# PSUM of a transformer stage as one tile of eight banks, and a new order of its steps

## The chip, the core and the metric

The kernel runs on one core of a Trainium2 chip. The core has TensorE (PE; its weight loads are shown apart as PEld), VectorE (DVE), ScalarE (ACT), GpSimd (POOL) and SyncE (SP, which here only issues DMAs). Each engine works through its own queue in order and waits on semaphores for the others. TensorE writes into PSUM, which has 8 banks of 512 float32 per partition; VectorE and ScalarE read it from there. The metric is the device time of one execution in microseconds, lower is better; it is given as the median of several runs.

## The reference, cut to what matters

Sixteen sequences of 256 tokens with 128 features go through two blocks. Block 0 is full attention, then a six-layer local transformer; block 1 is a state-space layer and a linear layer. The change lies in the local transformer:

```python
for i in range(DEPTH):                       # 6 layers
    x = attn_layer(shift_tokens(x), Wqkv[i], q_scale[i], k_scale[i], Wo[i]) + x
    x = ffn_layer(shift_tokens(x), ln_g[i], ln_b[i], W1[i], b1[i], W2[i], b2[i]) + x

def attn_layer(x, Wqkv, qs, ksc, Wo):        # 16 heads of 64
    q, k, v = heads(x @ Wqkv)
    q, k = rotary(l2norm(q) * qs), rotary(l2norm(k) * ksc)
    # a window of 32 queries sees its own 32 keys and the 32 before, masked
    return local_attention(q, k, v) @ Wo

def ffn_layer(x, g, bln, W1, b1, W2, b2):
    a, gate = split(layernorm(x) * g + bln) @ W1 + b1
    return a * gelu(gate) @ W2 + b2
```

`shift_tokens` delays half of the features by one token. All of it is float32.

## The kernel before

The tokens stay on the chip as `F`, features on the partitions. Class `Transformer` computes the six layers; a group is two sequences (512 tokens), so a layer has 8 groups and the stage 48. Work is cut into small steps, each a method that issues a few instructions on one engine. `ORDER` lists the steps of one period: `Pq00@0` is step P with the arguments q, 0, 0 for the period's own group, `FM2@3` is step FM with argument 2 for the group three periods earlier. `run` goes through this list once per group, so `ORDER` fixes the order of every engine's queue. `TAIL` lists by hand what is left after the 48th period, and the first steps of the state-space stage (`@s`), for which `Early` borrows the stage's tiles.

The steps, by engine. The arguments are q or k, the sequence b of the group, and the half t of its 256 tokens.

- TensorE. P (L628): q or k for 128 tokens, two matmuls of 512 columns. T (L702): transposes the rotated q or k, 16 pieces on 64 rows. X (L729): transposes F to tokens, as values. S (L759): scores, 64 small matmuls on 64 rows, added to the mask. G (L817): probabilities times values, 8 matmuls on 32 rows. Y (L838): four of the 16 heads times the product of Wv and Wo. F1, F5 (L858, L894): transposes round the layer norm. FP (L914) and FY (L938): the feed-forward matmuls. `value_output` (L608): makes the product of Wv and Wo of the next layer, half of it in each of a layer's last two periods, and copies it out with ScalarE.
- VectorE. C (L644) and N (L656): products with the cosine and sine tables, read from P's tile. R (L668): sums of squares. RR (L686): reciprocal. MX (L772) and SB (L778): maximum of the scores, and its subtraction. SM (L791): sums. TP (L805): transposes probabilities. FADD (L848), FF (L951), F2, FM: residual sums, statistics, gate. In the last layer FF has four more products (L960).
- ScalarE. Q (L638): squares of P's tile. E (L719): copies a transpose to SBUF. K (L746): writes the mask into the scores' tile. EX (L787): exponential. B (L828): copies G's result. W (L732): copies X's tile to SBUF. F4, F6, FE, SQ.
- POOL. A (L675): sum of C's and N's products. M (L690): times the reciprocal norm. NR (L798): times 1/sum. MXS, F3, FN.
- SP. V: two DMAs a sequence that shift the values by one window.

PSUM is shared out by two `Slots` objects: three tiles of two banks (`two`: for P, T, S, G, FP and `value_output`) and two of one bank (`one`: X, Y, F1, F5, FY). `take` gives the slot that has been free longest; `drop` counts a tile's readers and frees it after the last one. The instruction that writes a slot next waits for the last reader of the tile before.

Of the kernel before, what the change touches and what calls it, by code (L numbers as in the profile page):

```python
# [10 lines left out]
F32 = mybir.dt.float32  # L11
# [6 lines left out]
P = 128  # L18
B, S, D = 16, 256, 128
# [3 lines left out]
NG = B // G  # L23
# [8 lines left out]
DEPTH, HEADS, DH, W = 6, 16, 64, 32  # L32
PAIRS = HEADS // 2
INNER = HEADS * DH
FF = int(D * 4 * 2 / 3)
# [423 lines left out]


ORDER = """
Pq00@0 FM2@3 Cq00@0 Nq000@0 EX01@1 Mq10@1 Mk10@1 SM01@1 EX00@1 G10@2 Qq000@0 FADD0@2 B101@2 B100@2
Ak11@1 FY@3 Nq001@0 Aq00@0 SM00@1 Qq001@0 Rq00@0 G11@2 B111@2 FF@3 Mq11@1 X0@1 Pk01@0 Ck01@0 Tk10@1
B110@2 Pq01@0 Nk010@0 Nk011@0 W0@1 Ek10@1 Qk010@0 Cq01@0 Qk011@0 Pk00@0 Ak01@0 Tq10@1 V0@1 Qk000@0
Qk001@0 Nq010@0 Nq011@0 Aq01@0 NR00@1 Y10@2 Eq10@1 Y11@2 Qq010@0 Qq011@0 Rk01@0 Rk00@0 NR01@1 Ck00@0
K10@1 Nk000@0 Rq01@0 MXS0@0 Mk11@1 Tq11@1 Eq11@1 S10@1 Nk001@0 TP00@1 Ak00@0 Pq11@0 MX10@1 SB10@1
SQ0@0 Qq110@0 Nq110@0 Nq111@0 Cq11@0 Pq10@0 Qq100@0 Qq101@0 Tk11@1 Y12@2 Qq111@0 Nq100@0 Nq101@0
Cq10@0 Ek11@1 Y13@2 FADD1@2 G00@1 K11@1 B000@1 S11@1 TP01@1 B001@1 X1@1 G01@1 RR0@0 EX10@1 Aq10@0
MX11@1 Mk00@0 SB11@1 F1@2 F2@2 B010@1 B011@1 Mq00@0 W1@1 EX11@1 Rq10@0 Mq01@0 Pk10@0 Pk11@0 Qk110@0
Tk00@0 Ek00@0 F3@2 FN@2 F4@2 Ck10@0 Nk100@0 Nk101@0 Ck11@0 Aq11@0 V1@1 Y00@1 Tq00@0 Eq00@0 Y01@1  # L470
Tq01@0 F5@2 Qk100@0 Y02@1 Qk101@0 K00@0 SM11@1 F6@2 Mk01@0 SM10@1 S00@0 Eq01@0 Tk01@0 Rk10@0 Nk110@0
Nk111@0 NR11@1 TP11@1 Qk111@0 MX00@0 SB00@0 Ek01@0 FP0@2 FE0@2 Rk11@0 K01@0 FP1@2 NR10@1 Y03@1
Rq11@0 MXS1@0 FE1@2 FM0@2 FM1@2 Ak10@0 SQ1@0 TP10@1 RR1@0 S01@0 MX01@0 FP2@2 FE2@2 SB01@0
"""

TAIL = """
Ak11@0 Mk10@0 X0@0 FADD0@1 Mk11@0 W0@0 G10@1 FM2@2 L1@s B101@1 Mq11@0 G11@1 EX00@0 B110@1 B111@1  # L480
ST@s B100@1 Mq10@0 FY@2 Tq11@0 AG@s Tk10@0 Tk11@0 SM00@0 Eq11@0 Tq10@0 FF@2 Ek10@0 RS@s NB@s Y10@1
K11@0 Ek11@0 EX01@0 Y11@1 NR00@0 S11@0 V0@0 TP00@0 Y12@1 Eq10@0 SM01@0 MX11@0 Y13@1 XN@s L2@s SB11@0
K10@0 G00@0 FADD1@1 X1@0 EX11@0 SM11@0 S10@0 HT@s NR01@0 F1@1 B001@0 TP01@0 MX10@0 SB10@0 B000@0
NR11@0 W1@0 PX1@s U1@s G01@0 B010@0 PX0@s F2@1 B011@0 TP11@0 V1@0 Y00@0 F3@1 EX10@0 FN@1 Y01@0 G11@0
U0@s SM10@0 Y02@0 NR10@0 TP10@0 F4@1 Y03@0 PD@s B111@0 B110@0 XD@s WB@s G10@0 B100@0 B101@0 PZ1@s
F5@1 FADD0@0 ZA1@s F6@1 PZ0@s ZA0@s EE@s WW@s Y10@0 W2@s Y11@0 Y12@0 Y13@0 ZR1@s FADD1@0 FP0@1 F1@0
ZR0@s FP1@1 LL@s FP2@1 FE1@1 LW@s F2@0 FE0@1 F3@0 ZF@s FM1@1 FM0@1 FE2@1 FN@0 DU@s F4@0 FM2@1 F5@0
FY@1 F6@0 FP1@0 FP2@0 FP0@0 FE1@0 FF@1 FE2@0 TB@s FM1@0 FM2@0 FE0@0 FM0@0 FY@0 CB@s FF@0 MS@s
"""


class Slots:


    def __init__(self, pool, tag, n):
        self.pool, self.tag, self.free, self.held = pool, tag, list(range(n)), {}

    def take(self, shape, name, uses=1):
        i = self.free.pop(0)
        t = self.pool.tile(shape, F32, tag=f"{self.tag}{i}", name=name, bufs=1)  # L500
        self.held[id(t)] = [t, i, uses]
        return t

    def drop(self, t):
        h = self.held[id(t)]
        h[2] -= 1
        if h[2] == 0:
            self.free.append(h[1])
            del self.held[id(t)]


class Transformer:
# [36 lines left out]
    def pools(self, ctx, m):  # L549
        tc = self.c.tc  # L550
        self.m = m
        self.sb = ctx.enter_context(tc.tile_pool(name="lts", bufs=2))
        ps = ctx.enter_context(tc.tile_pool(name="ltp", bufs=1, space=PSUM))
        self.two = Slots(ps, "two", 3)
        self.one = Slots(ps, "one", 2)
        self.su, self.sw = Slots(self.sb, "u", 7), Slots(self.sb, "w", 4)
        self.spp, self.spT, self.sqT = (Slots(self.sb, k, 2) for k in ("pp", "pT", "qT"))

        self.kT = self.sb.tile([P, PAIRS, W + S], F32, tag="kT", name="kT", bufs=1)
        self.c.nc.gpsimd.memset(self.kT[:, :, 0:W], 0.0)  # L560
        self.at = self.sb.tile([P, HEADS, S], F32, tag="at", name="at", bufs=1)

        self.xw = []
        for b in range(G):
            t = self.sb.tile([P, NT, 2, D], F32, tag=f"xw{b}", name=f"xw{b}", bufs=1)
            self.c.nc.gpsimd.memset(t[0:W, 0, 0, :], 0.0)
            self.xw.append(t)
# [29 lines left out]
    def value_output(self, i, jh):  # L597

        nc, l = self.c.nc, self.layers[i]
        if jh == 0:  # L600
            l.wvo = self.wp.tile([P, HEADS, D], F32, tag="wvo", name="wvo")
        pw = self.two.take([P, 2, 4, D], "pw")
        for j in range(4):
            for e in range(2):
                es = slice(e * DH, (e + 1) * DH)
                jj = jh * 4 + j

                nc.tensor.matmul(  # L608
                    pw[:, e, j, :],
                    l.wv[es, jj, :],  # L610
                    l.wo[es, jj, :],
                    start=(j == 0),
                    stop=True,
                    skip_group_check=True,
                )
        for e in range(2):
            o = e * PAIRS + jh * 4
            nc.scalar.copy(l.wvo[:, o : o + 4, :], pw[:, e])
        self.two.drop(pw)
# [353 lines left out]
    def run(self):  # L973
        steps = []
        for o in ORDER.split():
            name, lag = o.split("@")
            base = name.rstrip("0123456789") if name[0] != "F" or name[:2] == "FA" else name
            steps.append((name, int(lag)))
        last = max(lag for _, lag in steps)
        groups = {}  # L980
        n = DEPTH * NG
        for jh in range(2):
            self.value_output(0, jh)
        for p in range(n):
            i, j = divmod(p, NG)
            if j == last + 1 and i + 1 < DEPTH:
                self.load(i + 1)
            if j >= NG - 2 and i + 1 < DEPTH:
                self.value_output(i + 1, j - NG + 2)
            if p == n - 4:  # L990
                self.early.load()
            groups[p] = self.group(p)
            for name, lag in steps:
                if p >= lag:
                    self.step(name, groups[p - lag])
            groups.pop(p - last, None)
        for o in TAIL.split():
            name, k = o.split("@")
            if k == "s":
                self.early.step(name)  # L1000
            else:
                self.step(name, groups[n - 1 - int(k)])
# [704 lines left out]
```

## Time and profile before

| | |
|---|---|
| runs | 3850.8, 3852.3, 3856.6 us; median 3852.29 |
| span of the profiled execution | 3847.4 us |
| mean granted TensorE clock | 0.987 |
| full attention, up to the first step of the local stage | about 430 us |
| 48 periods of the local stage | from about 430 to 3250 us |
| steady groups: 711.1 to 2946.1 us | 38 groups, PE busy 2217.0, DVE 2117.2, ACT 1711.0, POOL 1647.1 us |
| TAIL and the state-space stage | from 3250 us on |

The profile is one execution, with the start and the length of every instruction. A row of the timeline is start, length, engine, line, operation, output and inputs, shape, and how many equal instructions follow each other; in brackets stands idle time of the engine before it and what ended it. Lengths of TensorE rows are modelled and overlap, so the distance between the starts of two rows says more than the length of one. A float32 matmul leaves two MATMUL records and two weight loads, a transpose one of each. A row of waits is: engine, line, what it waited for, then microseconds in total, times, and the longest. "issue" stands for waiting for nothing that the profile shows.

### The profile page before, as it was taken

How to read it: one execution, taken by the hardware profiler on the slowest of the kernel's cores; microseconds unless marked ns; L12 is line 12 of the kernel's file. 1: busy time of each engine (PE TensorE's matmuls, PEld its weight loads, DVE VectorE, ACT ScalarE, POOL GpSimd, SP SyncE). 2: the span in 40 equal slices, each digit the busy share in tenths (PEclk: the TensorE clock that was granted, in tenths of full speed). 3: DMA queues.
4: the chain of work that ended last, by engine and by line, in shares of the span. 5: the costliest groups of instructions: out<-in, count | busy, mean ns of one | idle time of the engine just before them, and what ended most of it. 6: DMA issues, size and time to landing. Idle time of an engine off the chain costs nothing.

```text
span 3847.4 us, 104054 instructions
## 1 busy us (share of the span) xinstructions
PE 3693.1 (96%) x45040; PEld 2197.4 (57%) x45040; DVE 3385.9 (88%) x4736; ACT 2820.0 (73%) x4009; POOL 2603.6 (68%) x1636
## 2 busy tenths in 40 slices
PE   8999689999999999999999999999999999899997
PEld 4445355665655656666556656566665556555554
DVE  4665489999999999999999999999999999599997
ACT  3565467777777777777777777777777777689895
POOL 2222477777777777777777777777777776388887
PEclk9999789999999999999999999999999999999999
DMA  1000001000010000100001000010000000243432
GB/s 54 8 7 5 1 7 34 6 5 7 6 34 5 7 6 6 35 6 6 5 7 34 5 6 7 6 34 7 6 6 5 20 7 6 82 117 104 123 109 71
DMA packets 85669, 97.21 MB, mean 25 GB/s; under 512 B 9416, under 2 KB 56668, under 8 KB 84444
## 3 DMA queue, kind: packets, MB, share of 16 engines
q1 hardware_dynamic: 85212, 90.56, 8.5%
q8 instruction: 355, 5.82, 0.6%
q14 instruction: 102, 0.84, 0.1%
HBM read 75.32 MB, written 3.94 MB: 21 GB/s over the span
## 4 chain that ended last, share of the span: by engine, by line
PE 65%; DVE 20%; issue 2%; POOL 1%; ACT 1%; DVEq 0%; POOLq 0%; ACTq 0%
PE py L838 16%; PE pq L628 11%; PE pa L817 7%; PE fp L914 7%; PE s L759 6%; PE pt L702 5%; DVE w L656 3%; PE y L1361 3%; DVE u L644 3%; DVE ss L668 3%; PE db L1345 2%; DVE sm L791 2%; DVE s L1351 2%; PE px L1202 1%; DVE F L951 1%
## 5 line engine op out<-in xcount | busy, mean ns | idle before, releaser
L675 POOL TENSOR_TENSOR u<-u,w 128x1024 f32<-128x1024 f32 x384 | 907.2, 2367 | 405.2 <-DVE w L656 218.3
L690 POOL TENSOR_TENSOR u<-u,r 128x1024 f32<-128x1024 f32 x384 | 724.5, 1903 | 19.1 <-DVE r L686 16.6
L838 PE MATMUL py<-at,wvo 128*128 128x256 f32 x3072 | 736.5, 388 | 0.1
L628 PE MATMUL pq<-wqk,F 128*128 128x512 f32 x1536 | 715.6, 604 | 9.4 <-ACT sq L638 3.3
L638 ACT ACTIVATE sq<-pq 128x512 f32<-128x512 f32 x768 | 432.8, 601 | 301.3 <-PE pq L628 157.3
L838 PEld LDWEIGHTS py<-at,wvo 128*128 128x128 f32 x3072 | 569.6, 192 | 103.2 <-issue 23.2
L644 DVE TENSOR_TENSOR u<-pq,cosl 128x1024 f32<-128x1024 f32 x384 | 466.6, 1215 | 46.2 <-PE pq L628 43.1
L656 DVE TENSOR_TENSOR w<-pq,sinl 128x512 f32<-128x512 f32 x768 | 499.4, 681 | 8.9 <-ACT sq L638 2.1
L828 ACT COPY at<-pa 128x1024 f32<-128x1024 f32 x384 | 368.6, 1012 | 162.9 <-PE pa L817 157.9
L668 DVE TENSOR_REDUCE ss<-sq 128x16 f32<-128x1024 f32 x384 | 451.5, 1196 | 6.2 <-ACT sq L638 6.2
L628 PEld LDWEIGHTS pq<-wqk,F 128*128 128x128 f32 x1536 | 277.0, 191 | 296.2 <-issue 257.2
L817 PE MATMUL pa<-pT,xw 32*128 32x512 f32 x3072 | 411.8, 620 | 5.5 <-ACT sq L638 2.1
L798 POOL TENSOR_TENSOR pp<-pp,sm 128x1024 f32<-128x1024 f32 x192 | 363.8, 1916 | 50.3 <-DVE sm L794 50.3
L702 PEld LDWEIGHTS pt<-ident,u 64*128 64x128 f32 x6144 | 223.7, 139 | 227.0 <-issue 81.8
L1351 DVE TENSOR_TENSOR_SCAN s<-da,db 128x512 f32<-128x512 f32 x256 | 301.1, 1207 | 21.2 <-PE db L1345 9.3
L759 PEld LDWEIGHTS s<-kT,qT 64*32 64x32 f32 x24576 | 257.0, 106 | 90.0 <-issue 79.2
L759 PE MATMUL s<-kT,qT 64*32 64x64 f32 x24576 | 290.3, 227 | 16.4 <-issue 11.3
L702 PE MATMUL pt<-ident,u 64*128 64x64 f32 x6144 | 275.5, 230 | 29.4 <-ACT sq L638 10.6
L772 DVE TENSOR_REDUCE mx<-s 128x16 f32<-128x1024 f32 x192 | 230.5, 1200 | 69.7 <-PE s L759 67.2
L252 DVE TENSOR_REDUCE mx<-s 128x2 f32<-128x512 f32 x256 | 165.3, 687 | 139.9 <-PE sT L280 121.5
L817 PEld LDWEIGHTS pa<-pT,xw 32*128 32x128 f32 x3072 | 180.2, 186 | 172.6 <-issue 76.8
L914 PE MATMUL fp<-hT,w 128*128 128x512 f32 (+1 forms) x576 | 270.7, 606 | 0.0
(223 smaller groups left out, 6269.3 us busy)
## 6 DMA issues: line engine op xcount, KB each, us to landing
btd<-bc SPq DMA_DIRECT2D x72, 512.0 KB
bte<-bc SPq DMA_DIRECT2D x56, 256.0 KB
xw<-xw SPq DMA_DIRECT2D x96, 96.0 KB
wqk<-in_Wqk SPq DMA_DIRECT2D x6, 1024.0 KB
wv<-in_LWvT SPq DMA_DIRECT2D x6, 512.0 KB
wo<-in_Wo SPq DMA_DIRECT2D x6, 512.0 KB
xin<-in_x SPq DMA_DIRECT2D x8, 256.0 KB
out<-ot SPq DMA_DIRECT2D x8, 256.0 KB
```

What stands on the lines that cost most here:

```text
L628: nc.tensor.matmul(q.p[:, x], self.F[:, g.b0 + b, o : o + P], g.l.wqk[:, k, x, :], start=True, stop=True)
L638: self.c.nc.scalar.activation(q.sq[:, x], q.p[:, x], AF.Square)
L644: self.c.nc.vector.tensor_tensor(q.u.rearrange("p h x d -> p x h d"), q.p, g.l.cosl[:, t, k].unsqueeze(2).to_broadcast([P, 2, HEADS, DH // ...
L656: self.c.nc.vector.tensor_tensor(q.w[:, :, x], q.p[:, 1 - x], g.l.sinl[:, t, k, x, :].unsqueeze(1).to_broadcast([P, HEADS, DH // 2]), ALU. ...
L668: self.c.nc.vector.tensor_reduce(g.ss[b][:, t, k, :], q.sq.rearrange("p x h d -> p h x d"), AX.XY, ALU.add)
L675: self.c.nc.gpsimd.tensor_tensor(q.u, q.u, q.w, ALU.add)
L690: self.c.nc.gpsimd.tensor_tensor(uf, uf, g.r[b][:, t, k, :].unsqueeze(2).to_broadcast([P, HEADS, DH]), ALU.mult)
L702: self.c.nc.tensor.matmul(q.pt[:, r, j, :], uf[rs, j * P : (j + 1) * P], self.c.ident[rs, rs], is_transpose=True, start=(j == 0), stop=Tru ...
L759: nc.tensor.matmul(s[qs, e, j, :], qT[es, j, qs], kT[es, j, ks : ks + 2 * W], start=False, stop=True, skip_group_check=True,)
L817: self.c.nc.tensor.matmul(g.pa[b, t, w // 2][:, w % 2, :], self.xw[b][qs, t, k, :], g.pT[b, t][qs, k, :], start=(k == 0), stop=(k == 1),)
L838: self.c.nc.tensor.matmul(g.py[b], g.l.wvo[:, h, :], self.at[:, h, :], start=(h == 0), stop=(h == HEADS - 1),)
L914: self.c.nc.tensor.matmul(p[0:n, x, :], g.l.w1[:, w : w + n], g.hT, start=True, stop=True)
```

## The change

PSUM of the local stage becomes one tile of eight banks. A two-bank tile takes a free pair of banks (an even one and the next), the pair that has been free longest; a one-bank tile takes a free bank, by preference one whose neighbour is in use. `value_output` is split into its matmuls (step PW) and its copies (step PC), which get places in the order. `ORDER` and `TAIL` are new lists of the same steps: places within an engine's queue change, and seven steps change their lag (X0, W0 and Ak11 from 1 to 0, FADD0 from 2 to 1, FM2 from 3 to 2, FM0 from 2 to 3, RR1 from 0 to 1).

```diff
 ORDER = """
-Pq00@0 FM2@3 Cq00@0 Nq000@0 EX01@1 Mq10@1 Mk10@1 SM01@1 EX00@1 G10@2 Qq000@0 FADD0@2 B101@2 B100@2
...
-Cq10@0 Ek11@1 Y13@2 FADD1@2 G00@1 K11@1 B000@1 S11@1 TP01@1 B001@1 X1@1 G01@1 RR0@0 EX10@1 Aq10@0
-MX11@1 Mk00@0 SB11@1 F1@2 F2@2 B010@1 B011@1 Mq00@0 W1@1 EX11@1 Rq10@0 Mq01@0 Pk10@0 Pk11@0 Qk110@0
-Tk00@0 Ek00@0 F3@2 FN@2 F4@2 Ck10@0 Nk100@0 Nk101@0 Ck11@0 Aq11@0 V1@1 Y00@1 Tq00@0 Eq00@0 Y01@1
-Tq01@0 F5@2 Qk100@0 Y02@1 Qk101@0 K00@0 SM11@1 F6@2 Mk01@0 SM10@1 S00@0 Eq01@0 Tk01@0 Rk10@0 Nk110@0
-Nk111@0 NR11@1 TP11@1 Qk111@0 MX00@0 SB00@0 Ek01@0 FP0@2 FE0@2 Rk11@0 K01@0 FP1@2 NR10@1 Y03@1
-Rq11@0 MXS1@0 FE1@2 FM0@2 FM1@2 Ak10@0 SQ1@0 TP10@1 RR1@0 S01@0 MX01@0 FP2@2 FE2@2 SB01@0
+PW@0 PC@0 Pq00@0 G10@2 EX01@1 FM0@3 RR1@1 Nq000@0 Cq00@0 SM01@1 X1@1 Qq000@0 Qq001@0 Mk10@1 Nq001@0
+B101@2 Rq00@0 FY@3 B100@2 G11@2 EX00@1 B111@2 Pk01@0 B110@2 FF@3 SM00@1 Nk010@0 Qk010@0 W1@1 Pk00@0
+Mq11@1 Aq00@0 Mq10@1 Ck01@0 Tq10@1 Tk10@1 Nk011@0 Qk011@0 Qk000@0 Mk11@1 Ek10@1 Ak01@0 NR00@1 Pq01@0
+Nk000@0 Rk01@0 Ck00@0 Y10@2 Nk001@0 Eq10@1 Qq010@0 Y11@2 Cq01@0 Nq010@0 Qk001@0 Tq11@1 Nq011@0 K10@1
+Qq011@0 Rk00@0 NR01@1 Tk11@1 TP00@1 Eq11@1 Rq01@0 S10@1 V0@1 Pq10@0 MX10@1 MXS0@0 Y12@2 SQ0@0 Ek11@1
+RR0@0 SB10@1 V1@1 Nq100@0 Qq100@0 Y13@2 Ak00@0 Nq101@0 EX10@1 Aq01@0 Cq10@0 Mq01@0 FADD1@2 Pq11@0
+G00@1 TP01@1 Nq110@0 Qq101@0 K11@1 Qq110@0 S11@1 Aq10@0 Qq111@0 B000@1 Nq111@0 Tq01@0 Cq11@0 B001@1
+Mk01@0 Eq01@0 MX11@1 SB11@1 G01@1 SM10@1 F1@2 Mk00@0 X0@0 F2@2 B010@1 Rq10@0 W0@0 Mq00@0 B011@1
+Pk10@0 Qk100@0 Qk101@0 F3@2 EX11@1 Y00@1 Ck10@0 Nk100@0 Y01@1 FN@2 Nk101@0 Tq00@0 Tk00@0 Tk01@0 F4@2
+F5@2 Eq00@0 Ek00@0 F6@2 Pk11@0 Rk10@0 Aq11@0 Ek01@0 Ak10@0 SM11@1 FP2@2 Rq11@0 FP1@2 Nk110@0 Nk111@0
+FE2@2 Ck11@0 Y02@1 NR11@1 TP11@1 Qk110@0 Qk111@0 FM2@2 NR10@1 K00@0 K01@0 FE1@2 Rk11@0 S00@0 S01@0
+Y03@1 TP10@1 FM1@2 Ak11@0 MX00@0 MXS1@0 MX01@0 SQ1@0 SB00@0 SB01@0 FADD0@1 FP0@2 FE0@2
 """
...
+class Banks:
+    def __init__(self, t):
+        self.t, self.n = t, t.shape[1]
+        self.user, self.since, self.clock, self.held = [0] * self.n, list(range(self.n)), self.n, {}
...
+    def pair(self):
+        free = [b for b in range(0, self.n, 2) if not self.user[b] and not self.user[b + 1]]
+        return min(free, key=lambda b: max(self.since[b], self.since[b + 1]))
+
+    def single(self):
+        free = [b for b in range(self.n) if not self.user[b]]
+        split = [b for b in free if self.user[b ^ 1]]
+        return min(split or free, key=lambda b: self.since[b])
...
-        self.two = Slots(ps, "two", 3)
-        self.one = Slots(ps, "one", 2)
+        banks = Banks(ps.tile([P, 8, 512], F32, tag="banks", name="banks"))
+        self.two, self.one = Banked(banks, 2), Banked(banks, 1)
...
-            if j >= NG - 2 and i + 1 < DEPTH:
-                self.value_output(i + 1, j - NG + 2)
...
-                if p >= lag:
+                if name in ("PW", "PC"):
+                    if j >= NG - 2 and i + 1 < DEPTH:
+                        value = self.value_output if name == "PW" else self.value_output_copy
+                        value(i + 1, j - NG + 2)
+                elif p >= lag:
                     self.step(name, groups[p - lag])
```

`Banked` has `Slots`' interface (`take`, `drop`): it marks the banks that it takes as used and gives out a view of the one tile. `TAIL` has to finish what `ORDER` leaves over, so with the lags it loses Ak11@0, FADD0@1, FM2@2, W0@0 and X0@0 and gains FM0@2 and RR1@0; its other steps are those of before, in a new order.

On TensorE one period reads, before: Pq00 G10 FY G11 X0 Pk01 Tk10 Pq01 Pk00 Tq10 Y10 Y11 Tq11 S10 Pq11 Pq10 Tk11 Y12 Y13 G00 S11 X1 G01 F1 Pk10 Pk11 Tk00 Y00 Tq00 Y01 Tq01 F5 Y02 S00 Tk01 FP0 FP1 Y03 S01 FP2. After: (PW) Pq00 G10 X1 FY G11 Pk01 Pk00 Tq10 Tk10 Pq01 Y10 Y11 Tq11 Tk11 S10 Pq10 Y12 Y13 Pq11 G00 S11 Tq01 G01 F1 X0 Pk10 Y00 Y01 Tq00 Tk00 Tk01 F5 Pk11 FP2 FP1 Y02 S00 S01 Y03 FP0.

More of the change, by code (lines that the diff above doesn't have):

```diff
@@ L461 @@
 ORDER = """
-Pq00@0 FM2@3 Cq00@0 Nq000@0 EX01@1 Mq10@1 Mk10@1 SM01@1 EX00@1 G10@2 Qq000@0 FADD0@2 B101@2 B100@2
[L463 to L466, printed above, removed]
@@ L467 @@
-SQ0@0 Qq110@0 Nq110@0 Nq111@0 Cq11@0 Pq10@0 Qq100@0 Qq101@0 Tk11@1 Y12@2 Qq111@0 Nq100@0 Nq101@0
-Cq10@0 Ek11@1 Y13@2 FADD1@2 G00@1 K11@1 B000@1 S11@1 TP01@1 B001@1 X1@1 G01@1 RR0@0 EX10@1 Aq10@0
-MX11@1 Mk00@0 SB11@1 F1@2 F2@2 B010@1 B011@1 Mq00@0 W1@1 EX11@1 Rq10@0 Mq01@0 Pk10@0 Pk11@0 Qk110@0
-Tk00@0 Ek00@0 F3@2 FN@2 F4@2 Ck10@0 Nk100@0 Nk101@0 Ck11@0 Aq11@0 V1@1 Y00@1 Tq00@0 Eq00@0 Y01@1
-Tq01@0 F5@2 Qk100@0 Y02@1 Qk101@0 K00@0 SM11@1 F6@2 Mk01@0 SM10@1 S00@0 Eq01@0 Tk01@0 Rk10@0 Nk110@0
-Nk111@0 NR11@1 TP11@1 Qk111@0 MX00@0 SB00@0 Ek01@0 FP0@2 FE0@2 Rk11@0 K01@0 FP1@2 NR10@1 Y03@1
@@ L474 @@
+FE2@2 Ck11@0 Y02@1 NR11@1 TP11@1 Qk110@0 Qk111@0 FM2@2 NR10@1 K00@0 K01@0 FE1@2 Rk11@0 S00@0 S01@0
+Y03@1 TP10@1 FM1@2 Ak11@0 MX00@0 MXS1@0 MX01@0 SQ1@0 SB00@0 SB01@0 FADD0@1 FP0@2 FE0@2
 """
 TAIL = """
-Ak11@0 Mk10@0 X0@0 FADD0@1 Mk11@0 W0@0 G10@1 FM2@2 L1@s B101@1 Mq11@0 G11@1 EX00@0 B110@1 B111@1
-ST@s B100@1 Mq10@0 FY@2 Tq11@0 AG@s Tk10@0 Tk11@0 SM00@0 Eq11@0 Tq10@0 FF@2 Ek10@0 RS@s NB@s Y10@1
-K11@0 Ek11@0 EX01@0 Y11@1 NR00@0 S11@0 V0@0 TP00@0 Y12@1 Eq10@0 SM01@0 MX11@0 Y13@1 XN@s L2@s SB11@0
@@ L483 @@
[L483 to L487, printed above, removed]
@@ L488 @@
-FY@1 F6@0 FP1@0 FP2@0 FP0@0 FE1@0 FF@1 FE2@0 TB@s FM1@0 FM2@0 FE0@0 FM0@0 FY@0 CB@s FF@0 MS@s
+FM0@2 V0@0 G11@1 B111@1 B110@1 G10@1 B101@1 B100@1 L1@s FY@2 RR1@0 Mq10@0 Mk11@0 EX01@0 ST@s AG@s
+RS@s NB@s Mq11@0 Y10@1 FF@2 Y11@1 X1@0 EX00@0 Tq10@0 XN@s SM01@0 W1@0 V1@0 SM00@0 Mk10@0 NR01@0
+Tk10@0 Tq11@0 Eq11@0 Eq10@0 Ek10@0 TP01@0 L2@s HT@s NR00@0 Y12@1 Y13@1 FADD1@1 Tk11@0 G01@0 K10@0
+S10@0 Ek11@0 B011@0 TP00@0 G00@0 B010@0 K11@0 S11@0 B001@0 F1@1 MX10@0 SB10@0 EX10@0 SM10@0 MX11@0
+F2@1 F3@1 FN@1 B000@0 PX0@s U0@s NR10@0 PX1@s Y00@0 U1@s PD@s SB11@0 EX11@0 Y01@0 SM11@0 NR11@0
@@ L489 @@
+TP11@0 XD@s WB@s Y02@0 Y03@0 TP10@0 F4@1 G11@0 FADD0@0 G10@0 B110@0 TB@s F5@1 B111@0 B100@0 CB@s
+B101@0 PZ1@s ZA1@s PZ0@s ZR0@s ZA0@s EE@s F6@1 WW@s LL@s Y10@0 W2@s Y11@0 Y12@0 LW@s Y13@0 FADD1@0
+FP1@1 F1@0 F2@0 F3@0 ZR1@s ZF@s FP2@1 FE2@1 FE1@1 FP0@1 FM1@1 FE0@1 FN@0 F4@0 F5@0 FM0@1 FM2@1 FY@1
+FF@1 F6@0 FP2@0 FE2@0 FP1@0 FE1@0 FM1@0 DU@s MS@s FP0@0 FE0@0 FM2@0 FM0@0 FY@0 FF@0
 """
@@ L509, in drop, with view, __init__, take @@
             del self.held[id(t)]
+class Banks:
+    def __init__(self, t):
+        self.t, self.n = t, t.shape[1]
+        self.user, self.since, self.clock, self.held = [0] * self.n, list(range(self.n)), self.n, {}
+    def view(self, b, n, shape):
+        t = self.t[0 : shape[0], b : b + n, :].rearrange("p b x -> p (b x)")[:, 0 : int(np.prod(shape[1:]))]
+        if len(shape) > 2:
+            names = "abc"[: len(shape) - 1]
+            keys = dict(zip(names, shape[1:]))
+            t = t.rearrange(f"p ({' '.join(names)}) -> p {' '.join(names)}", **keys)
+        return t
+    def pair(self):
[5 more added lines that the diff above has]
+        return min(split or free, key=lambda b: self.since[b])
+class Banked:
+    def __init__(self, banks, n):
+        self.banks, self.n = banks, n
+    def take(self, shape, name, uses=1):
+        k = self.banks
+        b = k.pair() if self.n == 2 else k.single()
+        for i in range(b, b + self.n):
+            k.user[i] = 1
+        t = k.view(b, self.n, shape)
+        k.held[id(t)] = [t, b, uses]
+        return t
+    def drop(self, t):
+        k = self.banks
+        h = k.held[id(t)]
+        h[2] -= 1
+        if h[2] == 0:
+            for i in range(h[1], h[1] + self.n):
+                k.user[i], k.since[i] = 0, k.clock
+            k.clock += 1
+            del k.held[id(t)]
 class Transformer:
@@ L601, in value_output @@
             l.wvo = self.wp.tile([P, HEADS, D], F32, tag="wvo", name="wvo")
-        pw = self.two.take([P, 2, 4, D], "pw")
+        pw = l.pw = self.two.take([P, 2, 4, D], "pw")
         for j in range(4):
@@ L615, in value_output, with value_output_copy @@
                 )
+    def value_output_copy(self, i, jh):
+        nc, l = self.c.nc, self.layers[i]
+        pw = l.pw
         for e in range(2):
@@ L983, in run @@
             self.value_output(0, jh)
+            self.value_output_copy(0, jh)
         for p in range(n):
```

## The prediction

> **What bounds the kernel now.** I read the page first (shares and queues), then the busy time of each engine in a steady stretch of the local stage, the chain of waits over one group, the timeline of TensorE, and last the waits.
>
> ```profile
> PE 3693.1 (96%) x45040; PEld 2197.4 (57%) x45040; DVE 3385.9 (88%) x4736; ACT 2820.0 (73%) x4009; POOL 2603.6 (68%) x1636
> ...
> PEclk9999789999999999999999999999999999999999
> ...
> q8 instruction: 355, 5.82, 0.6%
> ```
>
> The reader is to see a TensorE at full clock that is never idle, a VectorE not far behind it, and a queue that carries instructions: 90,080 matmuls and weight loads in 355 packets (5.82 MB, so 16.4 KB each); one packet is some 254 of them (the built program has 91,052 with its waits: 256 each).
>
> The busy times from 1000 to 1290.5 us (five groups) are PE 287.9, DVE 275.3, ACT 221.7, POOL 216.0: per group 57.6, 55.1, 44.3, 43.2. A group takes 58.1: the `u` product of step Cq00 starts at 2829.8 and, two groups later, at 2946.1.
>
> ```profile
> 1002.92 1.73 PE pq L628 x4
> 1004.67 1.23 DVE u L644
> ...
> 1025.35 1.12 DVE mx L772
> 1026.49 1.24 DVE pp L778
> 1027.86 0.28 PE pt L702 x2
> ...
> 1061.23 1.73 PE pq L628 x4
> 1062.99 1.22 DVE u L644
> ```
>
> This is the chain of waits. It is a loop: 23.2 us of VectorE (Cq00 to SB10, 1004.67 to 1027.86), then 35.1 us of TensorE (Tk11 to the next Pq00). The hand-over back is a PSUM wait: Tk11 needs a two-bank tile, and the third is held by the scores that SB10 reads. TensorE is almost full by itself: that wait costs it only 0.2 us a group (`pt <- DVE pp` below).
>
> ```profile
> 1018.23 3.72 PE L838 MATMUL py<-at,wvo 128*128 128x256 f32 x16
> 1043.00 2.00 PE L838 MATMUL py<-at,wvo 128*128 128x256 f32 x8
> 1044.93 0.71 PE L702 MATMUL pt<-ident,u 64*128 64x64 f32 x16
> 1048.63 1.89 PE L838 MATMUL py<-at,wvo 128*128 128x256 f32 x8
> ...
> 1550.04 1.42 PE L759 MATMUL s<-kT,qT 64*32 64x64 f32 x120
> 1552.91 0.32 PE L759 MATMUL s<-kT,qT 64*32 64x64 f32 x8 [1.45 <-issue]
> ```
>
> ```profile
> PE s L759 <- issue: 8.5, 8, 1.8
> PE pt L702 <- DVE pp L778: 4.8, 21, 0.2
> ```
>
> Two things are to be seen. Changing the array's shape costs time: 16 `py` records between two transposes last 3.65 us (1018.23 to the next start, 1021.88), 8 last 1.93 (1043.00 to 1044.93). So 8 more cost 1.72, and the two ends of such a stretch 1.93 - 1.72 = 0.21. And TensorE sometimes stops inside a run of scores with nothing to wait for but its next instructions. At 1552.91 a packet of q8 had started at 1550.52 and landed at 1551.60; and the stop, after 240 of the run's 256 instructions, is at a multiple of 256 of TensorE's program (instruction 239 of the run).
>
> **The change, part by part.** I use S for scores, T for transposes, G, Y, P, FP as the steps are named; "full" is a matmul on the whole array (P, X, Y, FY, F1, F5, FP), "split" one on 64 or 32 rows (T, S, G).
>
> *PSUM as eight banks.* No compute instruction is added. In the built program TensorE's separate waits fall from 903 to 460, VectorE's rise from 633 to 734, ScalarE's from 579 to 641, POOL's from 673 to 765. Such a wait is an EVENT_SEMAPHORE row of 28 ns (median of ten before L732): 101 x 0.028 = 2.8 us on VectorE over the whole run, off the path while VectorE has 3 us free a group. Tk11 no longer waits for SB10 (in the new program it waits for Nq011, Qq011 and Mk11): -0.2 us a group.
>
> *The order on TensorE.* Same matmuls, but the full ones stand together. Before, a group has 13 stretches of full work between split work: FP2-Pq00, FY, X0-Pk01, Pq01-Pk00, Y10-Y11, Pq11-Pq10, Y12-Y13, X1, F1-Pk10-Pk11, Y00, Y01, F5-Y02, FP0-FP1-Y03. After, 7: Y03-FP0-Pq00, X1-FY, Pk01-Pk00, Pq01-Y10-Y11, Pq10 to Pq11, F1 to Y01, F5 to Y02. 6 x 0.21 = -1.26. Split steps next to each other (T beside S: 0.64 and 1.41 whatever stands next; T beside G isn't in the trace) I cost at nothing; bounds -0.1 and +0.25, the gap between the slow and fast G (1.93 and 2.18). TensorE alone would then need 58.1 - 0.2 - 1.26 = 56.6 us a group.
>
> *The order on the others.* VectorE's 55.1 stay. The moves (FADD0, RR1 and the FM/FP steps change places and lags, X0 and W0 go to the group's own period) add no instruction. V0's and V1's two DMAs still have SP's queue to themselves; W0 now stands some 20 us of TensorE work ahead of V0. The longest loop through several engines that I find in the new order is MX01, SB01 and on to Nq110 on VectorE (32.4), Qq111 and B000 on ScalarE (2.4), Tq01 to S01 on TensorE (20.8): 55.6. So nothing but TensorE binds, with 1 us to spare, and that 1 us hides every other edit; if it goes, VectorE's gaps (2.4 us a group now) come on top.
>
> *What the new order costs: the supply of instructions.* S00 and S01 now follow each other: 128 matmuls, 512 instructions, in 2.82 us. Any 512 hold a whole block of 256, gone in 1.41 us. From the packets and matmul starts in the trace: deep in a run of scores, the next packet starts 0.9 us after a block's first instruction and lands at 2.0, and after the stops TensorE resumes 1.4 after landing. That is 3.3 us against 1.41: a stop of 1.9. The seven large ones between 660 and 3000 us were 1.3 to 1.8 (mean 1.56, their block held a few transposes as well). Where a block starts within about 9 matmuls of the run's begin, the packet starts 0.8 us before it, and S00, S01 and S11 show no stop over 0.4. Laying out the new program's instructions in blocks, the first boundary is deeper than 9 matmuls in 40 of the 47 groups after the first: (40 x 1.65 + 7 x 0.4) / 47 = +1.46 a group; 1.65 lies between the trace's mean and 1.9. T-T-S10 is a run of 320; in 13 of 47 groups a boundary falls in its transposes, a block lasts 1.45 to 2.2, a stop is 3.3 less that, about 1.3: 13 x 1.3 / 47 = +0.36. The stops of now go: 7 x 1.56 / 40 = -0.27. Sum +1.55. TensorE has no idle time that could take it in.
>
> [...]
>
> *Steady groups:* -0.2 - 1.26 + 1.55 = +0.1 us, over the 38 groups from 711 to 2946 about +2. The `pw` matmuls of ten of them (1.4 us each, 59.5 against 58.1) stay; their copies move to ScalarE's first place, where it has 14 us a group free.
>
> *Last layer.* FF there has four more products on VectorE (`xT`, L960, 2.05 us); the groups from 2946 to 3192 take 61.4. In the new order the loop above becomes 55.6 + 2.05 + 1.65 = 59.3, TensorE 58.2; I take 59.4: five groups x -2.0 = -10, bounds 0 and -15.
>
> *Filling and TAIL.* The first groups wait for POOL and ScalarE (longest single wait 4.0), the last chain from 3253 to 3333 is mostly TensorE. Neither order takes work out of them. I take 0, bounds of two such waits either way, -8 and +8.
>
> Sum: +2 - 10 + 0 = -8 us against the execution's 3847.4. The median of the runs is 3852.3, 4.9 above it with what lies around the span; so 3844.
>
> **Rivals.**
>
> *The instructions come in time (the whole gain).* For it: from 660 to 3000 us S00 and S01, each alone after full work, never stopped. Against it: all rows with a block begun deep in a run. Then 38 x -1.46 - 10 = -66: 3786.
>
> *Slower: two starved blocks a group.* At S00-S01 the stop is the full 1.9 in every group, and the T-T-S10 run stops in every second group by as much, because the waits on Nq011 and Mk11 keep TensorE from running ahead. Stops 1.9 + 0.95 - 0.27 = 2.58; 2.58 - 1.46 = +1.12 x 43 = +48, less the 10: 3890. It decides from 1.75 us of stops a group. For it: S10 is where nearly all stops are now. Against it: only 13 boundaries in 47.
>
> *The one PSUM tile is tracked as one.* Then every take would wait for all eight banks and TensorE and VectorE would alternate, 57.6 + 55.1 a group, some 2400 us more. Against it: the new program's waits name single steps.
>
> **How the numbers follow.** Forecast (gain and starvation about even, 3818 to 3866): 0.50. Whole gain: 0.15. Two starved blocks: 0.33. One tile: 0.02. About 0.2% (7.7 us) is what a measurement of this kernel tells from no change. The forecast's range splits 0.26 / 0.14 / 0.10 into faster, same, slower; with the rivals faster 0.41, same 0.14, slower 0.45. The range leaves out 0.10 below (the deepest part of the whole gain) and 0.10 above: 3792 to 3893.
>
> **What would show it.** Right: `pt <- DVE pp` gone from TensorE's waits; `py` stretches with one pair of ends; a stop of 1.3 to 1.9 at `s` L759 after `issue` in about every group, 60 to 90 us in all; a group at 58.0 to 58.9; last layer under 60. Wrong: `issue` under 20 us in all (whole gain), over 110 (two blocks), or TensorE waiting for `sq`, `at` or `mx`, which would mean the 55.6 us loop is longer than I found.

## The result, and the profile after

The changed kernel took 3868.3 us (median of 4 runs, 3860.1 to 3873.9), the kernel before beside it 3851.6: a ratio of 1.0045, 95% interval 1.0029 to 1.0061. It is slower by about 17 us, where 8 us less was forecast. The profiled executions are 19.3 us apart (3847.4 and 3866.7).

From the page after: busy time of the engines, the queue that carries instructions, and the shares of the chain that ended last. All PSUM tiles are named `banks` now, and lines lie 56 further down (L815 is step S, L684 P, L758 T, L873 G, L894 Y, L712 N, L1016 the `xT` products of FF, L746 the POOL step M).

```profile
PE 3619.4 (94%) x45040; PEld 2183.0 (56%) x45040; DVE 3379.3 (87%) x4736; ACT 2815.7 (73%) x4007; POOL 2605.5 (67%) x1636
...
q8 instruction: 353, 5.78, 0.6%
...
PE 77%; DVE 6%; issue 4%; ACT 1%; POOL 1%; DVEq 0%; POOLq 0%; ACTq 0%
```

TensorE is busy 74 us less in a span that is 19 us longer: the time went into its idle gaps, and "issue", 2% of the chain before, is 4%. Its waits in the local stage (from 560 to 3260 us), in total us, times and the longest:

```profile
PE banks L815 <- issue: 86.1, 49, 2.5
PE banks L684 <- DVE w L712: 21.3, 5, 4.9
```

Before, in the same stretch, the scores' `issue` was 10.9 us, and the waits of `pt` for `DVE pp` and `ACT sq` 5.4 and 8.9; both are gone. So the PSUM waits went as they should, and two things came: 49 stops of the scores, and five waits of P for VectorE.

To see where each lies I take the start of step FY's first matmul in each of the groups (L938 before, L994 after) and subtract:

| profiled execution, us | to the first FY | next 40 groups (one) | next 5 groups (one) | the rest | span |
|---|---|---|---|---|---|
| before | 595.5 | 2352.4 (58.81) | 311.1 (62.2) | 588.5 | 3847.4 |
| after | 597.9 | 2356.4 (58.91) | 324.1 (64.8) | 588.3 | 3866.7 |
| difference | +2.5 | +4.0 | +13.0 | -0.2 | +19.3 |

The steady groups stand where they were, to 0.1 us a group. As the table divides it, two thirds of the loss lie in the five groups of the last layer; but the steady row is a gain and losses that nearly cancel, as the next paragraphs show.

**The steady groups.** The timeline after, at the two S steps that now follow each other (start, length, engine, line, operation, tiles, shape, how many; in brackets idle time before and its reason):

```profile
2064.03 2.51 PE L815 MATMUL banks<-kT,qT 64*32 64x64 f32 x233
2068.49 0.42 PE L815 MATMUL banks<-kT,qT 64*32 64x64 f32 x23 [1.95 <-issue]
```

A run of 256 records; after 233 of them TensorE stands still for 1.95 us and waits for nothing that the profile shows. Counted in TensorE's own program, the record at which it stops is at a multiple of 256 instructions, here and in every one of the 44 groups from the fourth to the last but one. In 42 of them it lies inside the run, and the distance between the two starts is 1.6 to 2.7 us, 2.1 on average; in the other two it is the first record of Y03, just behind the run, after 1.4 and 1.6 us of idling.

Some of these stops cost clock as well. Three stretches of 3.41 us, the first with a stop of 1.99 us in it (after the comma the busy times of PE, PEld, DVE, ACT and POOL, at the end TensorE's granted clock, the DMA share and GB/s):

```profile
702.07:705.48 3.41, 1.42 (x140) 1.27 (x131) 2.44 (x3) 3.23 (x4) 0.00 (x0) 1.00 0.02 5
705.48:708.90 3.42, 3.42 (x71) 2.80 (x65) 2.35 (x3) 0.00 (x0) 0.00 (x0) 0.50 0.02 5
708.90:712.31 3.41, 3.41 (x11) 1.82 (x10) 2.74 (x6) 1.76 (x2) 0.00 (x0) 1.00 0.02 5
```

Before, the 40 groups have the full clock throughout. After, it is at half for 3.41 us twelve times, 41 us in all, each time behind such a stop. The price can be read from three executions whose 40 groups hold the same work (this one, and the two runs below that move `xT` or read it from PSUM): 19 groups have a half-clock stretch in one of them and none in another, and with it the same group is 1.2 to 2.0 us longer, 1.6 on average, the scores themselves left out. So an estimate of what it costs the 40 groups is 12 x 1.6 = 19 us.

**The last layer.** The timeline again, VectorE's `xT` products with POOL's step M beside them, and P, which waits for the PSUM pair that `w` still reads:

```profile
3088.14 3.94 POOL L746 TENSOR_TENSOR u<-u,r 128x1024 f32<-128x1024 f32 x2
...
3088.75 4.64 DVE L1016 SCALAR_TENSOR_TENSOR xT<-F,m0mod,xT 64x256 f32<-64x256 f32 x4
...
3096.70 1.28 DVE L712 TENSOR_TENSOR w<-banks,sinl 128x512 f32<-128x512 f32 x2
...
3097.43 3.04 PE L684 MATMUL banks<-wqk,F 128*128 128x512 f32 x4 [4.09 <-DVE w L712]
```

The four products take 4.64 us, not the 2.02 of before. Single ones: 1.56 and 2.01 for the first two, 0.48 and 0.48 for the others. The first begins 0.61 us after a 1.89 us M and ends 0.28 after M's end; the second begins 0.35 after the next M (2.08) and ends 0.28 after it; then POOL is idle. In all five groups the first two take 1.56 to 1.65 and 2.01 us, and each of the ten ends 0.28 us after POOL's instruction: they are held until it is over. The hand-over comes late by that much, TensorE idles 4.1 to 4.9 us, and what follows is slow as well. The busy time in four stretches round one such wait:

```profile
3010.00:3028.00 18.00, 18.00 (x201) 9.38 (x188) 15.81 (x20) 10.26 (x14) 9.99 (x5) 1.00 0.13 43
3028.00:3033.00 5.00, 0.19 (x8) 0.05 (x2) 4.84 (x9) 0.50 (x2) 0.00 (x0) 0.70 0.02 4
3033.00:3037.00 4.00, 3.88 (x6) 1.79 (x7) 3.52 (x5) 3.78 (x7) 3.79 (x2) 0.53 0.00 0
3037.00:3060.00 23.00, 22.79 (x392) 15.29 (x391) 21.53 (x33) 16.96 (x22) 18.09 (x11) 1.00 0.03 8
```

After the gap the clock is granted at 0.53 for 4 us: the four records of P take 3.57 us from start to start (3033.12 to 3036.69); at full clock they take 1.82 (a row below shows it).

The half clock is not new here. Before, four of these five groups have a stretch of 3.41 us of it (13.7 us in all, after: 23.9), each behind a wait of T for `sq` of 1.84 or 1.85 us:

```profile
2960.89 0.71 PE L702 MATMUL pt<-ident,u 64*128 64x64 f32 x16 [1.85 <-ACT sq L638]
2961.54 5.41 PE L838 MATMUL py<-at,wvo 128*128 128x256 f32 x16
2966.88 0.71 PE L702 MATMUL pt<-ident,u 64*128 64x64 f32 x16
```

The 16 `py` records last 5.34 us from start to start, where the prediction's rows have 3.65.

Both inputs of the held products, `F` and `xT`, lie in SBUF; whether that matters is tried below. In the traces of before and after every stretch of half clock in the local stage lasts 3.41 us or a multiple of it, and the idling ahead of it can be short: in the gap above TensorE fell idle at 3028.19 and the half clock began at 3029.96, 1.8 us later, and before it followed a wait of 1.85. In the ten traces of this case, from 600 to 3260 us, every fall to half follows a stretch of 3.41 us in which TensorE was idle for 1.71 us or more, and none fails to follow where it was idle for more than 1.91.

### The profile page after: what moved, and what is told of

Read it like the earlier page. It is cut to its first block, busy times and chain, and to the rows that moved or that the text cites. A ratio compares the mean times of both kernels' runs of the same rounds, so it can differ in the third digit from the quotient of the medians.

```text
span 3866.7 us, 103864 instructions
## 1 busy us (share of the span) xinstructions
PE 3619.4 (94%) x45040; PEld 2183.0 (56%) x45040; DVE 3379.3 (87%) x4736; ACT 2815.7 (73%) x4007; POOL 2605.5 (67%) x1636
## 4 chain that ended last, share of the span: by engine, by line
PE 77%; DVE 6%; issue 4%; ACT 1%; POOL 1%; DVEq 0%; POOLq 0%; ACTq 0%
PE banks L894 18%; PE banks L684 17%; PE banks L873 9%; PE banks L815 7%; PE banks L970 6%; PE banks L758 5%; PE y L1420 3%; PE banks L994 3%; PE db L1404 2%; DVE s L1410 2%; PE px L1261 1%; PE banks L950 1%; PE banks L914 1%; DVE xT L1016 1%; PE banks L785 1%
## 5 line engine op out<-in xcount | busy, mean ns | idle before, releaser
L746 POOL TENSOR_TENSOR u<-u,r 128x1024 f32<-128x1024 f32 x384 | 723.8, 1907 | 468.9 <-DVE r L742 465.2
L684 PE MATMUL banks<-wqk,F 128*128 128x512 f32 x1536 | 739.9, 610 | 23.6 <-DVE w L712 21.3
L894 PE MATMUL banks<-at,wvo 128*128 128x256 f32 x3072 | 726.0, 388 | 3.2 <-issue 3.0
L894 PEld LDWEIGHTS banks<-at,wvo 128*128 128x128 f32 x3072 | 590.1, 194 | 178.1 <-issue 65.6
L694 ACT ACTIVATE sq<-banks 128x512 f32<-128x512 f32 x768 | 435.2, 599 | 268.2 <-DVE u L700 159.2
L712 DVE TENSOR_TENSOR w<-banks,sinl 128x512 f32<-128x512 f32 x768 | 496.3, 677 | 68.8 <-PE banks L684 61.0
L700 DVE TENSOR_TENSOR u<-banks,cosl 128x1024 f32<-128x1024 f32 x384 | 466.2, 1214 | 10.2 <-ACT sq L694 6.1
L884 ACT COPY at<-banks 128x1024 f32<-128x1024 f32 x384 | 375.6, 1021 | 104.8 <-PE banks L873 104.5
L684 PEld LDWEIGHTS banks<-wqk,F 128*128 128x128 f32 x1536 | 274.2, 192 | 301.5 <-issue 249.4
L873 PE MATMUL banks<-pT,xw 32*128 32x512 f32 x3072 | 395.1, 616 | 4.2 <-issue 2.2
L815 PE MATMUL banks<-kT,qT 64*32 64x64 f32 x24576 | 289.4, 228 | 101.4 <-issue 91.5
L815 PEld LDWEIGHTS banks<-kT,qT 64*32 64x32 f32 x24576 | 257.0, 106 | 165.2 <-issue 124.5
L873 PEld LDWEIGHTS banks<-pT,xw 32*128 32x128 f32 x3072 | 150.9, 184 | 199.8 <-issue 121.2
L758 PEld LDWEIGHTS banks<-ident,u 64*128 64x128 f32 x6144 | 208.7, 140 | 96.8 <-POOL u L746 58.5
```

What stands on the lines that cost most here:

```text
L684: nc.tensor.matmul(q.p[:, x], self.F[:, g.b0 + b, o : o + P], g.l.wqk[:, k, x, :], start=True, stop=True)
L694: self.c.nc.scalar.activation(q.sq[:, x], q.p[:, x], AF.Square)
L700: self.c.nc.vector.tensor_tensor(q.u.rearrange("p h x d -> p x h d"), q.p, g.l.cosl[:, t, k].unsqueeze(2).to_broadcast([P, 2, HEADS, DH // ...
L712: self.c.nc.vector.tensor_tensor(q.w[:, :, x], q.p[:, 1 - x], g.l.sinl[:, t, k, x, :].unsqueeze(1).to_broadcast([P, HEADS, DH // 2]), ALU. ...
L746: self.c.nc.gpsimd.tensor_tensor(uf, uf, g.r[b][:, t, k, :].unsqueeze(2).to_broadcast([P, HEADS, DH]), ALU.mult)
L758: self.c.nc.tensor.matmul(q.pt[:, r, j, :], uf[rs, j * P : (j + 1) * P], self.c.ident[rs, rs], is_transpose=True, start=(j == 0), stop=Tru ...
```

## The experiments

My theory of the result: a run of 512 score instructions outruns their supply, in every group; and in the last layer `xT` meets POOL. The rivals: the new loop through VectorE binds and the stops only fill its slack; the last layer is slow from filling and draining.

**Y03 between S00 and S01.**

```diff
-... FE1@2 Rk11@0 S00@0 S01@0
-Y03@1 TP10@1 ...
+... FE1@2 Rk11@0 S00@0 Y03@1
+S01@0 TP10@1 ...
```

> The changed kernel with step Y03 between S00 and S01. Theory (instructions come late in a run of 512): the stop of about 1.9 us in the second half of the scores, now in every group, goes; one more pair of array changes (0.21). Steady groups 58.9 -> about 57.3 (40 x -1.6 = -64), TensorE's waits for issue at the scores from 91 us to under 20. The last layer stays near 64.8 a group, since S01 ends where it did (Y03 takes the stop's place) and VectorE's part of that loop is as it was. Total 3868 - 65 = about 3803. Rival (the loop S01, MX01, SB01, VectorE to Nk010, Pq01 binds the steady groups, the stop only fills its slack): no gain, 3860 to 3868.

Measured: 3841.9 us, ratio to the kernel before 0.9982 (0.9973 to 0.9990). 40 groups took 2323.9 us, 32.5 less; the next five 325.6, as expected unchanged. TensorE's waits from 560 to 3260 us:

```profile
PE banks L684 <- DVE w L712: 24.6, 5, 4.9
PE banks L684 <- DVE pp L834: 19.0, 35, 0.6
PE banks L815 <- issue: 10.0, 14, 1.9
```

The stops fell from 86 to 10 us. So they came from the length of the run. No half clock is left in the 40 groups either, which the expectation had not counted. But only half of the gain arrived: a new wait of 19.0 us (and 5.6 of the `pw` matmuls) for `pp`, step SB. The rival was right in this much, that a wait stood behind the stop. Pq00 takes the pair that SB00 frees, and on VectorE SB00 stands behind MX01, which waits for S01.

**SB00 ahead of MX01 as well.**

```diff
-MX00@0 MXS1@0 MX01@0 SQ1@0 SB00@0 SB01@0
+MX00@0 SB00@0 MXS1@0 MX01@0 SQ1@0 SB01@0
```

> The kernel with Y03 between S00 and S01, and SB00 ahead of MX01 on VectorE. In the kernel with Y03 alone moved Pq00 waited 0.5 us in 45 groups for SB00 (24.6 us), because MX01, which waits for S01, stood ahead of SB00. Theory: that wait took the rest of the gain; it goes, steady groups 58.1 -> 57.5, total 3842 - 24 = about 3818. Rival (the loop through MX01, SB01, Nk010 and Pq01 has no slack left and takes the wait over): TensorE waits for DVE w instead, total 3835 to 3842.

Measured: 3800.9 us, 0.9869 (0.9855 to 0.9883); 40 groups 2288.6 us, 57.22 each. From 560 to 3260 us:

```profile
PE banks L684 <- DVE w L712: 24.1, 5, 4.9
PE banks L815 <- issue: 8.8, 11, 1.9
```

The wait for `pp` is gone, and none took its place. The steady groups fell by 35 us where 24 were expected, so the wait's own row was not all that it cost (the start-to-start distances from FP to P or `pw` fell by 27 us).

**xT as a step of its own.** The four products are taken out of FF into a step XT, called where VectorE waits for scores and POOL is idle; in `TAIL` it follows each FF at once.

```diff
-... FM1@2 Ak11@0 MX00@0 ...
+... FM1@2 Ak11@0 XT@3 MX00@0 ...
```

> The changed kernel with the four products of the last layer (xT) as a step of their own just ahead of MX00, where VectorE waits for scores and POOL is idle. Theory (the products stand still beside POOL's M, VectorE hands over late, TensorE idles over 4 us and then runs at half clock): four products 0.48 each, TensorE's 4 us waits for the sine products gone, last-layer groups 64.8 -> 58.3 to 59, five groups x -6 = -30, total about 3838, under the kernel before. Rival (the last layer is slow because the new order is slow to fill or to drain): under 8 us gained.

Measured: the five groups took 295.2 us instead of 324.1 (-28.9, expected -30), and the waits for `DVE w` are gone. The products in this kernel:

```profile
3063.15 1.96 DVE L1019 SCALAR_TENSOR_TENSOR xT<-F,m0mod,xT 64x256 f32<-64x256 f32 x4
3065.14 2.36 DVE L828 TENSOR_REDUCE mx<-banks 128x16 f32<-128x1024 f32 x2
```

1.96 us for four, and the maximum of the scores follows without a pause. (In the first of the five groups the first product met a POOL instruction after all and took 1.35.) The half clock in the five groups, 23.9 us after, is gone with the waits. The median, though, is 3849.0 us, ratio 1.0001 (0.9991 to 1.0011): 19 below the changed kernel, not 30. Its runs lie between 3840.6 and 3858.8, and the profiled one is the fastest. The mean granted clock goes with the time: 0.979 to 0.982 in the seven runs above 3848 us, 0.983 or 0.984 in four of the five below 3844 (0.980 in the fifth). That fits more stretches of half clock in the slower runs; no profile of one shows it.

**xT from PSUM, in its old place.** One input in SBUF instead of two, everything else as after; F's old value is missing from `xT`.

```diff
-xb, src, self.m[p, 5, bi : bi + 1], xb, ALU.mult, ALU.add
+xb, g.f[p, b, :], self.m[p, 5, bi : bi + 1], xb, ALU.mult, ALU.add
```

> The changed kernel with the four products in their place, but reading the feed-forward result in PSUM in place of F in SBUF: the same size and count, one input in SBUF in place of two; the residual is left out of xT. Theory (two SBUF inputs have to wait for POOL's running instruction): four products 0.48 each, VectorE 2.65 sooner, TensorE's wait 4.1 -> about 1.5, no half clock after it (another 2.1), last-layer groups 64.8 -> about 60, total about 3844. Rival (the products wait for data or for a semaphore, or it is 2.05 us of work in this place that costs): still 1.6 and 2.0 us for the first two, total 3860 or more.

The products of this kernel (min, median and max in ns), and P after its wait:

```profile
L1015 DVE SCALAR_TENSOR_TENSOR xT<-banks,m0mod,xT x32: 475/484/492, 2971.3 to 3346.0; 64x256 f32<-64x256 f32 x32
```

```profile
3040.27 1.98 PE L684 MATMUL banks<-wqk,F 128*128 128x512 f32 x4 [2.11 <-DVE w L712]
3042.09 3.19 PE L894 MATMUL banks<-at,wvo 128*128 128x256 f32 x14
```

None of the 32 is held up; TensorE's wait is 2.1 us at most (7.5 in all five) and P runs at full speed after it, 1.82 us. The five groups took 305.9 us, 18.2 less than after; expected were 24. Same place, same count, same size: the hold-up is a matter of where the second input lies (0.49 us at most, against 2.02 after). The total was no proof: 3859.2 us, just short of the rival's 3860, as the steady groups of this run took 10 us more than after (5 of them at the scores; 47.8 us of half clock in place of 41). The half clock behind P's wait was taken away together with the long wait, so its share was not tried by itself; 6.8 us of it are left in the five groups, behind stops of the scores.

**The eight-bank tile alone**, with the old `ORDER` and `TAIL`:

```diff
-        self.two = Slots(ps, "two", 3)
-        self.one = Slots(ps, "one", 2)
+        banks = Banks(ps.tile([P, 8, 512], F32, tag="banks", name="banks"))
+        self.two, self.one = Banked(banks, 2), Banked(banks, 1)
```

> The kernel before with the eight-bank PSUM tile alone, ORDER and TAIL as they were. Prediction's step: Tk11 no longer waits for SB10, -0.2 us a group: 3842 to 3852. Rival (the waits on one tile that the scheduler has to spell out cost more, or first steps meet other banks): slower by 5 us or more.

A miss, on the good side: 3827.4 us, 0.9948 (0.9935 to 0.9961). And not by the wait I had named:

```profile
PE banks L753 <- DVE pp L829: 14.6, 43, 1.5
PE banks L810 <- issue: 3.3, 4, 1.4
PE banks L889 <- ACT sq L689: 3.1, 5, 0.7
```

T still waits for `pp`, longer than before (14.6 us against 5.4). What fell is the scores' `issue` (10.9 to 3.3) and the wait for `sq` in the last layer (8.9 to 3.1). 40 groups took 9.4 us less, which is the scores' own loss, since the distances between successive score records sum to 205.4 us instead of 215.0; the five groups took 6.1 less and the start 6.3 less. With the wait for `sq` at 0.7 us or less there is no half clock in the five groups, where before had 13.7 us of it.

The same kernel again, to see whether the stops stay away:

> The kernel before with the eight-bank tile alone, once more, one look: the scores' stops of the kernel before (9.5 us in the steady groups) were gone in the first profile. If that hangs on addresses, they are gone again and the span is 3825 to 3832.

3832.4 us, span 3830.6; 40 groups 2343.3, five groups 304.6, and 1.7 us of `issue` at the scores from 600 to 2950. The first two and the stops repeat; the start does not (594.1 instead of 589.2). Why the stops are fewer is open. In the kernel before one separate wait stands between Tq11 and S10 in TensorE's program, here none, and where S10 begins within 32 instructions of a block's start the packet starts 0.3 to 0.8 us after S10's first matmul before, and between 3.8 us ahead of it and 0.1 after it here. That agrees with the wait holding back the packet; it wasn't tried by itself.

The opposite part, the new order with the old two pools, can't be had: at one point the new order needs more tiles than three and two.

**The kernel before with XT ahead of MX00.**

> The kernel before with the four xT products ahead of MX00. There they take 0.48 us each and meet no POOL work, but FF lies in the loop from Cq00 to SB10: last-layer groups 61.4 -> 59 at best, five groups -12, total 3850 - 12 = 3838. Rival (what is slow there is the filling of TAIL's steps): no gain.

Measured: 3847.1 us, 0.9995 (0.9985 to 1.0005); five groups 302.9 us instead of 311.1 (-8.2, expected -12), the rest as it was. There the products are not held up. What the move is worth was not split up: the four products are 2.02 us a group by themselves, but the wait for `sq` (8.9 us) and the 13.7 us of half clock behind it are gone too, and waits of 6.5 us of G have come.

**All three together** (Y03 between the S steps, SB00 early, XT).

> The same with the four xT products ahead of MX00 as well. Theory (last layer: lock and clock, 30 us, apart from the rest): last five groups from about 325 to 292 us, total about 3818 - 31 = 3787. Rival (with the shorter period VectorE has no room for 2 us more ahead of MX00): last five groups over 300, total over 3797.

("Lock" is the hold-up of the products beside POOL.) 3772.8 us, 0.9796 (0.9782 to 0.9809): faster than both kernels. 40 groups 2289.8 us, five groups 296.3 (321.2 without XT). Its page, and its waits on TensorE from 560 to 3260 us:

```profile
PE 3618.3 (96%) x45040; PEld 2174.1 (58%) x45040; DVE 3369.4 (89%) x4736; ACT 2814.3 (75%) x4007; POOL 2602.4 (69%) x1636
```

```profile
PE banks L815 <- issue: 10.6, 16, 2.1
PE banks L684 <- issue: 3.5, 3, 1.8
PE banks L873 <- DVE pp L834: 2.5, 5, 1.2
```

The same TensorE work as after (3618 us busy) in 94 us less; no sum over 10.6 us is left among its waits there.

## Why the prediction was wrong

Step by step, against the rows.

*PSUM, -0.2 us a group.* Right for the whole change: `DVE pp` is gone from TensorE's waits. Wrong for the part: with the tile alone the wait grew, and the tile brought 20 us by other ways.

*Array changes, -1.26, and the supply of instructions, +1.55.* Both have the right sign and both are too small. The distances between successive score records sum to 215.0 us before and 290.4 after in the 40 groups: +1.89 a group. All else fell from (2352.4 - 215.0) / 40 = 53.44 to (2356.4 - 290.4) / 40 = 51.65: -1.79, where -1.46 was forecast for the array changes and the PSUM wait together. This is a remainder: no run tried the array changes alone, and it has the half clock in it (about 0.48 a group by the estimate above), so that the gain itself was nearer -2.3. I had let 7 of 47 groups go without a stop, since S00 and S01, alone, showed none when a block began near the run's start; in a run of 512 the next block comes 256 instructions later all the same, and all 44 groups stopped. The stops were 2.1 us from start to start on average, not 1.65. Against that the T-T-S10 runs, forecast at 13 stops, had few: five stops of 0.9 to 1.2 us at scores other than S01's. The net was forecast at +0.1 us a group and is +0.10 (the 38 groups should have made that 3.4 us in the sum, not 2). That is luck: a gain larger than forecast, stops larger than forecast, and a clock that has no term. Of TensorE's waits for `issue` from 560 to 3260 us after, 86.1 us lie at the scores and 5.3 at all other lines: nearly all of this idling is at the scores.

*The clock, put at nothing.* The prediction took TensorE to be at full clock, from slices of the page that are 96 us wide. The trace of before had the half clock in the last layer, behind waits of 1.8 us, and the new order was to bring stops of that length into the steady groups. By the estimate above they cost 19 us there, as much as the whole loss.

*Last layer: five groups x -2.0 = -10, bounds 0 and -15.* This is the step that failed: it makes 23 of the 27 us between the sum (-8) and the profiled execution (+19.3). Measured +13.0. I had priced the four `xT` products at 2.05 us, from rows of before in which no POOL instruction ran beside them, and carried that duration to a place where POOL's M runs. There they take 4.64. The price of the place stood in the trace of before, in a row that I didn't read: an instruction of VectorE with both inputs in SBUF, on 4 elements a partition.

```profile
L870 DVE TENSOR_TENSOR frs<-fmv,eps x48: 161/620/634, 570.8 to 3313.4; 128x4 f32<-128x4 f32 x48
```

0.16 us where POOL is idle (3 times), mostly 0.62 where its step M runs (45 times, 0.44 to 0.63), each of these ending 0.02 us or so after POOL's instruction. Its minimum beside its median was the warning. From there it went on: in a steady group the `w` that P waits for ends 0.33 us before P starts (2084.77 + 0.68 against 2085.78), so that nearly all of the 4.64 us became idle time of TensorE, 4.08 us and more, with more half clock behind it. The bounds excluded it, because I looked for what the new order makes late and not for what it puts side by side.

*Filling and TAIL, 0 (-8 to +8).* +2.5 and -0.2: right.

The rivals. The whole gain was worth having: with the S steps apart and SB00 early the steady groups come to 57.22. "Two starved blocks" gave the right sign at 3890; one half of it came, a stop of some 2 us in every group, the other, stops of the T-T-S10 run in every second group, did not. "Nothing but TensorE binds, with 1 us to spare" held for the steady groups, with 0.33 us to spare, until the stops went; then SB00 behind MX01 bound at once.

## What to carry to other kernels

An instruction's duration belongs to its place (a product of 0.48 us took up to 2.02 beside POOL): before moving one, look at what the other engines run beside the new place, and take a line whose median is far above its minimum as a price list. A long run of tiny matmuls can be bounded by how fast its instructions arrive, as here (a stop of 2.1 us on average in a run of 512), so break it with work that lasts, and look again for what the stop had covered. Look at the granted clock in stretches of a few us and not in fortieths of the span: a stop can cost nearly as much again behind it (here an estimated 1.6 us behind stops of about 2). Try the parts of a change alone: here the tile alone was worth 20 us, and the order made for it gave all of that back and more.

## What was not expected of the hardware

- An elementwise product of 0.48 us took up to 2.02 us beside a POOL instruction when both its inputs were in SBUF, and 0.48 to 0.49 in all 32 cases with one of them in PSUM.
- Half the clock does not need a long gap: 1.7 to 2.3 us of idling within a stretch of 3.41 us brought it in twelve of the 40 steady groups, at some 1.6 us each beside the stop itself. Behind the idle gap of 4.9 us four records took 3.57 us for 1.82; behind one gap of 2.1 us the same four took 1.82.
- 44 runs of 512 score instructions met 44 stops, each at a multiple of 256 instructions, 42 of them inside the run, for 1.6 to 2.7 us.
